# Three graph layers on one core: the subset counts of a table lookup move behind the lookups, on half of the array's rows, with their bias as a row of ones

## The chip, the cores and the metric

The kernel runs on one core of a Trainium2 chip. The metric is the device time of one execution in microseconds (us); lower is better. A core has five engines with a queue of instructions each: TensorE (PE in the profile; its weight loads are PEld), VectorE (DVE), ScalarE (ACT), GpSimd (POOL) and SyncE (SP). An engine takes its own instructions in order and waits on semaphores for the others.

## The reference

A batch of 16 graphs with 1024 nodes and 128 features goes through four layers, each followed by a residual sum and a layer norm.

```python
x = _layernorm(x + _L0_gnn_ref(x, adj, ...))   # masked attention
x = _layernorm(x + _L1_gnn_ref(x, adj, W, b))  # largest edge message
x = _layernorm(x + _L2_gnn_ref(x, adj, ...))   # sum over neighbours, two-layer network
x = _layernorm(x + _L3_gnn_ref(x, adj, ...))   # edges thinned row by row, three convolutions
```

The change lies in layer 1. There every node i wants, for each of 128 features, the largest q over its neighbours j:

```python
p = jnp.einsum('bnd,do->bno', x, W1 - W2)
q = jnp.einsum('bnd,do->bno', x, W2)
pre = p[:, :, None, :] + q[:, None, :, :] + b
h = jax.nn.relu(pre) * adj[..., None]
return jnp.max(h, axis=2)
```

## The kernel before

**The lookup.** The 1024 possible neighbours of a graph are cut into groups of six (`GS`). For each group the kernel holds a table with the largest q of each of the 64 subsets of the group. For a node, the subset that its edges pick is found as a one-hot column of 64, and a product of the table with that column looks the value up. Two groups (a pair, `PS` = 12 neighbours) share the 128 rows. A graph has 86 pairs (`NP`). One pair is a *slot*, and a slot has two *half slots*, one for each 512 nodes. 16 graphs make 1376 slots and 2752 half slots; they are the main loop, and everything else of layers 0 to 2, and the thinning of edges for layer 3, is fitted in between as background work.

**One half slot** (`slot`, lines 849 to 892) issues, in this order of the program:

- `look_up` (L830): four products on TensorE for this slot. Each uses 64 of the 128 rows of the array: rows 0 to 63 for one group, 64 to 127 for the other. First both products with the table's `high` part, then both with its `low` part (a value is the sum of two parts). They fill a tile `pg`, of which there are two.
- the background: `dilate_on` and `advance` emit pieces of other streams on TensorE, then on ScalarE, VectorE and GpSimd. A planner with costs and due times (`ROOM`, `ask`) chooses them.
- `low_part` (L819), in the first half of odd slots only: a product that subtracts `high` from the exact table in the tile `pt`; ScalarE then copies `low` out (L821).
- `count` for two slots ahead (L799, L800): a product of the pattern `lit` (+1 and -1) with the 120 rows of adjacency columns `AT` counts, for each of 64 subsets, how well a node's edges fit it; ScalarE makes the one-hot `hot` of it with a Relu whose bias is `one_less` (L800).
- `table` (L811, L814), in the second half of even slots only: two transposes put the next two tables into `pt`, and ScalarE copies `high` out.
- VectorE's `tensor_max` (L890): the running largest value, over the 1024 looked-up elements of each partition.

The order is written out by hand for TensorE, ScalarE, VectorE and GpSimd (`manual_schedule`), so each engine executes what is named above in the order in which the program names it.

**Tiles that matter.** `pm` (a count) and `pt` (a table) share one tag of PSUM with two buffers, `subset`: every new `pm` or `pt` waits until the last but one has been read. From an even slot on the sequence is pm, pm, pt, pm, pm, so the second count of an odd slot takes the buffer that `pt` leaves, and `pt` is left when ScalarE has copied `low`. `AT` has four buffers of 120 rows in fp8; GpSimd issues the load of a chunk (120 columns of adjacency, ten slots' worth) two chunks ahead.

Of the kernel before, what the change touches and what calls it, by code (L numbers as in the profile page):

```python
# [29 lines left out]
F32 = mybir.dt.float32  # L30
F32R = mybir.dt.float32r
BF = mybir.dt.bfloat16
F8 = mybir.dt.float8e4
F16 = mybir.dt.float16
AF = mybir.ActivationFunctionType
# [4 lines left out]
B, N, D, H2 = 16, 1024, 128, 256  # L40
P = 128
T = N // P
GS = 6
PS = 2 * GS
PC = 10
CH = PC * PS
NP = -(-N // PS)
TG = 12
R, G = 32, 4
# [11 lines left out]
def subset_tables():  # L61

    half = P // 2
    s = np.arange(half)
    lit = np.zeros((CH, PC, P), np.float32)
    for j in range(CH):
        a, k = divmod(j % PS, GS)
        lit[j, j // PS, a * half:(a + 1) * half] = np.where((s >> k) & 1, 1.0, -1.0)
    size = sum((s >> k) & 1 for k in range(GS))
    return lit, np.tile(1.0 - size, 2).astype(np.float32).reshape(P, 1)  # L70


@with_exitstack
def tile_graph_layers(ctx: ExitStack, tc, a, out):
    nc = tc.nc
    x, adj, adjT = a["x"], a["adj"], a["adjT"]
    halves = (slice(0, 512), slice(512, 1024))

    consts = ctx.enter_context(tc.tile_pool(name="consts", bufs=1))
# [7 lines left out]
    def bank(name, dtype=F32):  # L87
        return psum.tile([P, 2048 // (2 if dtype == BF else 4)], dtype, tag="bank", name=name, bufs=2)
# [13 lines left out]
    nc.vector.memset(ones_b, 1.0)  # L102
    mhalf = consts.tile([P, T], F32, name="mhalf")
    nc.vector.memset(mhalf, -0.5)
    lit = consts.tile([CH, PC, P], F8, name="lit")
    nc.gpsimd.dma_start(out=lit, in_=a["lit"])
    less = consts.tile([P, P], F32R, name="less")
    nc.vector.tensor_scalar_mul(less, ident, -1.0)
    one_less = consts.tile([P, 1], F32, name="one_less")
    nc.sync.dma_start(out=one_less, in_=a["one_less"])  # L110

    def weight(name, shape=(P, P), how=None, pool=consts):
        t = pool.tile(list(shape), F32, name="w_" + name)
# [49 lines left out]
    pm = bank("pm")  # L163
# [5 lines left out]
    for b in range(B):  # L169
        q, g = divmod(b, G)  # L170
        nc.gpsimd.dma_start(out=half_rows[g * R:(g + 1) * R, :, q],
                            in_=a["nodemask"][b].rearrange("(k r) -> r k", r=R))
# [65 lines left out]
    def layers_012():  # L238
# [4 lines left out]
        apool = es.enter_context(tc.tile_pool(name="apool", bufs=1))  # L243
# [18 lines left out]
        def ask(engine, cost, take=False, give=False, same=False, delay=0.5, after=None, third=False, urgent=False):  # L262
            return engine, cost, take, give or urgent and None, 0 if same else delay, after, third
# [17 lines left out]
        def columns_of(dst, src, first=0.5):  # L281
            for h in range(2):
                yield ask("PE", 0.44, take=True, delay=0.5 if h else first)
                p = shared("ptr")
                for t in range(4):
                    nc.tensor.transpose(p[:, t * P:(t + 1) * P], src[:, 4 * h + t, :], ident)
                yield ask("A", 0.59, give=True, same=True)
                nc.scalar.copy(dst[:, halves[h]], p)
# [12 lines left out]
        def scores(b):  # L301
# [50 lines left out]
            yield from columns_of(xT, X[b])  # L352
            q = w4.tile([P, NP * PS], F32, name="q", bufs=2)
            nc.gpsimd.memset(q[:, N:], LOWEST)
# [104 lines left out]
        def tables_of(b):  # L459

            if b:
                yield ask("V", 0, urgent=True, after=("tables", b - 1))
            for g0 in range(0, NP, TG):
                n_g = 2 * min(TG, NP - g0)
                yield ask("V", 0.01, same=True, urgent=True, after=("q", b))
# [23 lines left out]
        def dilation():  # L489
# [134 lines left out]
            for k in range(K):  # L624
# [52 lines left out]
                for g in range(G):  # L677
                    nc.sync.dma_start(out=hit_p[g * R:(g + 1) * R],
                                      in_=hit_d.rearrange("(q g) n m -> g n q m", g=G)[g])
                yield (B * NP - 10) / K - 34.43, 0, False  # L680
                hit_T = dil.tile([P, Q, R], BF, name="hit_T")
# [62 lines left out]
        def load_columns(at):  # L744
            b, c = divmod(at, T + 1)
            if b < B:
                rows = min(CH, N - c * CH)
                t = AT[at] = apool.tile([CH, N], F8, name="AT", bufs=4)
                if rows < CH:
                    nc.gpsimd.memset(t, 0.0)  # L750
                nc.gpsimd.dma_start(out=t[:rows], in_=adjT[b, c * CH:c * CH + rows])

        An, AT, subs, qs, ps, values, exps, bests, hots, tables = ({} for _ in range(10))
        now, taken, given, held = 0, 0, {}, {}
        pending = {}
# [6 lines left out]
        def start(stream, first=False):  # L762
            pending[stream] = [next(stream, None), -9]
            streams.insert(0 if first else len(streams), stream)
# [27 lines left out]
        def count(s, h):  # L792

            b, g = divmod(s, NP)
            c, r = divmod(g, PC)
            if h == 0:
                hots[s] = w2.tile([P, N], F32R, name="hot", bufs=3)
            pm = psum.tile([P, 512], F32, tag="subset", name="pm", bufs=2)
            nc.tensor.matmul(pm, lit[:, r, :], AT[b * (T + 1) + c][:, halves[h]], start=True, stop=True)  # L799
            nc.scalar.activation(hots[s][:, halves[h]], pm, AF.Relu, bias=one_less)  # L800

        def table(s):

            b, g = divmod(s, NP)
            g0 = g - g % TG
            assert ("sub", b, g0) in happened, (s, [(x.__name__, pending[x]) for x in streams], room)
            pt = psum.tile([P, 512], F32, tag="subset", name="pt", bufs=2)[:, :2 * P]
            if g + 2 - g0 == min(TG, NP - g0):
                happened["used", b, g0] = now
            for k in range(2):  # L810
                nc.tensor.matmul(pt[:, k * P:(k + 1) * P], subs[b, g0][:, g - g0 + k, :], ident, is_transpose=True,  # L811
                                 start=(k == 0), stop=(k == 1))
            high = w2.tile([P, 2 * P], F32R, name="high", bufs=2)
            nc.scalar.copy(high, pt)  # L814
            tables[s] = pt, high
# [8 lines left out]
        def look_up(s, h, pg):  # L824

            at = s % 2
            for k, part in enumerate(tables[s - at]):
                for a in range(2):
                    rows = slice(64 * a, 64 * a + 64)
                    nc.tensor.matmul(pg[:, a], part[rows, at * P:(at + 1) * P], hots[s][rows, halves[h]],  # L830
                                     start=(k == 0), stop=(k == 1))
# [17 lines left out]
        def slot(s, last):  # L849

            nonlocal now
            now = s
            b, g = divmod(s, NP)
            if s >= 0 and g == 0:
                finish(b)
                if b + 1 < B:
                    start(tables_of(b + 1), True)
                    load_x(b + 1)
                    start(attend(b + 1))
                    start(scores(b + 1))  # L860
                if b:
                    start(rest(b - 1))
            if s >= 0 and g % PC == 0:
                load_columns(b * (T + 1) + g // PC + 2)
            for h in range(2):
                now = s + 0.5 * h
                for e in ROOM:
                    room[e] = min(room[e] + ROOM[e] / 2, ROOM[e])
                if s >= 0:
                    pg = psum.tile([P, 2, 512], F32, tag="wide", name="pg", bufs=2)  # L870
                    look_up(s, h, pg)
                early = s >= 0 and due < now
                if early:
                    dilate_on()
                advance(("PE",))
                advance(("A", "V", "Pool"))
                if s >= 0 and not early:
                    dilate_on()
                if h == 0 and s % 2 and s + 1 < last:
                    low_part(s + 1)  # L880
                if s + 2 < last:
                    count(s + 2, h)
                    if h and s % 2 == 0:
                        table(s + 2)
                if s >= 0:
                    own = bests[b][:, :, halves[h]]
                    if g == 0:
                        nc.vector.tensor_copy(own, pg)
                    else:
                        nc.vector.tensor_max(own, own, pg)  # L890
            if s >= 0:
                hots.pop(s)
# [1 line left out]
        dilate = dilation()  # L894
        due, wants_bank = 0.0, False
        load_x(0)
        for at in range(2):
            load_columns(at)
        front, back = scores(0), attend(0)
        for t in range(T):  # L900
            while ("e", 0, t) not in happened:
# [6 lines left out]
        first = tables_of(0)  # L908
# [9 lines left out]
        last = rest(B - 1)  # L918
# [214 lines left out]
    for b in range(B):  # L1133
        x0 = sb.tile([P, T, D], F32, name="h", bufs=2)
        nc.sync.dma_start(out=x0, in_=x3[b])
        part = load_share(b)
        m = expanded(ahead[b][0])
        transposed(R3[b], x0)
        r = sage(b, convolve(x0, m, part), R3[b], None, weights)
        if b + 1 < B:  # L1140
            start = len(nc.cur_bb.bb.instructions)
# [15 lines left out]
    r = second(0)  # L1157
    for b in range(B):
        near = ep.tile([P, T, N], F8, name="near", bufs=2)
        nc.sync.dma_start(out=near, in_=kept[b])  # L1160
        part = load_share(b)
        following = second(b + 1) if b + 1 < B else None
        pass_on(b, 1, r, expanded(near), part, stats)
        r = following
# [3 lines left out]
    r = second(0)  # L1168
    for b in range(B):
        following = second(b + 1) if b + 1 < B else None  # L1170
        columns(b, r, stats)
        r = following
# [16 lines left out]
    o = summed(0)  # L1189
    for b in range(B):  # L1190
# [17 lines left out]
        o = following  # L1208
# [25 lines left out]
```

## Time and profile before

| | |
|---|---|
| time, median of 3 runs | 6459.39 us (6446.67 to 6460.74) |
| the profiled execution's own time | 6458.95 us |
| its span, and around it | 6457.2 us; 1.75 us |
| main loop, first lookup to last comparison | 132 to 5169 us of the span |
| granted TensorE clock, mean of the span | 0.934 |
| L890 `best<-best,pg` on DVE | 2720 times, mean 1215 ns |
| L800 `hot<-pm,one_less` on ACT | 2752 times, mean 689 ns |
| L799 `pm<-AT,lit` on PE | 2752 times, mean 404 ns |
| L830 `pg<-hot,high` and `pg<-hot,low` on PE | 5504 times each, mean 519 and 411 ns |

The profile comes from one execution. A TensorE row's duration runs from its start to the end of its results; the next product begins before that, so what a product costs in a row of products is the distance from its start to the next start.

### The profile page before, as it was taken

To read this page: it belongs to the slowest core of one execution; us is meant where nothing else is said; L and a number is where in the kernel's file an instruction comes from. 1 tells how busy PE (TensorE), PEld (TensorE's weight loads), DVE (VectorE), ACT (ScalarE), POOL (GpSimd) and SP (SyncE) were. 2 spreads that over 40 slices of the span, in tenths; PEclk is the share of its full clock that TensorE was granted. 3 is DMA by queue.
4 is the path that set the end of the run, shared out by engine and by line. 5 is a ranking of instruction groups with operands and counts; after the bars stand their busy time and mean duration, and the time that the engine had idled before them with its cause. 6 is when DMAs were issued, how large, how long until landed. Compare 5 with 4: busy or idle time off the path is not lost. (4 is left out here: it accounts for less than half of the span.)

```text
span 6457.2 us, 90620 instructions
## 1 busy us (share of the span) xinstructions
PE 5729.3 (89%) x29184; PEld 2962.2 (46%) x29354; DVE 4978.8 (77%) x7877; ACT 3946.3 (61%) x7142; POOL 3502.1 (54%) x11319
## 2 busy tenths in 40 slices
PE   6989999989899999999989998989998867877998
PEld 3444444444444444444444444444443335555654
DVE  3888888888888888888888888888888834444445
ACT  4667666666667666766666666666665623333755
POOL 2665766666666666766666666666666511110113
PEclk8989899999899999999999999998998988888999
DMA  5121212121212121212121212121211065654545
GB/s 38 13 30 21 35 21 36 21 34 21 34 21 37 20 35 20 34 20 32 24 34 20 34 20 34 20 35 20 35 21 18 20 101 106 126 103 111 206 167 186
DMA packets 478402, 317.32 MB, mean 49 GB/s; under 512 B 301162, under 2 KB 429668, under 8 KB 473828
## 3 DMA queue, kind: packets, MB, share of 16 engines
q0 software_dynamic: 105648, 84.20, 15.0%
q1 hardware_dynamic: 367600, 226.13, 11.9%
q8 instruction: 230, 3.77, 0.2%
q10 hardware_dynamic: 4676, 1.19, 0.1%
q14 instruction: 248, 2.03, 0.1%
HBM read 412.71 MB, written 117.18 MB: 82 GB/s over the span
## 5 line engine op out<-in xcount | busy, mean ns | idle before, releaser
L890 DVE TENSOR_TENSOR best<-best,pg 128x1024 f32<-128x1024 f32 x2720 | 3258.7, 1215 | 556.8 <-PE pg L830 546.8
L800 ACT ACTIVATE hot<-pm,one_less 128x512 fp32r<-128x512 f32 x2752 | 1882.7, 689 | 736.9 <-PE pm L799 727.5
L830 PE MATMUL pg<-hot,high 64*128 64x512 f32 x5504 | 1436.1, 519 | 239.2 <-DVE best L890 231.4
L830 PE MATMUL pg<-hot,low 64*128 64x512 f32 x5504 | 1139.8, 411 | 0.0
L799 PE MATMUL pm<-AT,lit 120*128 120x512 fp8e4 x2752 | 1110.3, 404 | 20.9 <-ACT hot L800 8.5
L830 PEld LDWEIGHTS pg<-hot,high 64*128 64x128 f32 x5504 | 533.6, 191 | 1018.9 <-DVE best L890 510.5
L830 PEld LDWEIGHTS pg<-hot,low 64*128 64x128 f32 x5504 | 553.0, 198 | 0.0
L658 POOL TENSOR_SCALAR sc<-low_counts,half_mask,rest 16x1 f32<-16x1 f32 x992 | 351.8, 355 | 323.7 <-DVE rest L644 218.8
L799 PEld LDWEIGHTS <-lit 120*128 120x128 fp8e4 x2752 | 272.6, 99 | 520.5 <-issue 460.2
L663 POOL TENSOR_SCALAR sc<-sc 16x1 f32<-16x1 f32 x992 | 397.3, 401 | 105.1
L821 ACT CAST low<-pt 128x256 fp32r<-128x256 f32 x688 | 256.1, 372 | 258.2 <-PE pt L819 255.0
L1039 POOL TENSOR_TENSOR length<-length,mhalf 128x8 f32<-128x8 f32 x48 | 78.9, 1644 | 570.8 <-DVE length L1038 570.8
L660 POOL TENSOR_SCALAR sc<-sc 16x1 f32<-16x1 f32 x992 | 315.0, 318 | 107.7
L819 PE MATMUL pt<-high,less 128*128 128x256 f32 x688 | 294.1, 427 | 85.0 <-ACT high L814 78.2
L703 POOL TENSOR_SCALAR shifts<-centre 128x4 f32<-128x4 f32 x32 | 10.5, 327 | 656.9 <-DVE width L699 633.6
L665 POOL TENSOR_SCALAR hit<-V,sc 16x31 bf16<-16x31 bf16 (+30 forms) x992 | 361.1, 364 | 0.0
L666 POOL TENSOR_SCALAR last_rank<-V,sc 16x31 f32<-16x31 bf16 (+30 forms) x992 | 344.5, 347 | 0.0
L996 ACT CAST m<-near 128x1024 fp32r<-128x1024 fp8e4 x256 | 253.4, 1044 | 112.6 <-DVE near L965 59.6
L475 DVE TENSOR_TENSOR sub<-sub,q 128x24 f32<-128x24 f32 (+11 forms) x768 | 303.3, 396 | 24.0 <-ACT q L297 10.4
L811 PE MATMUL pt<-ident,sub 128*128 128x128 f32 x1376 | 286.1, 291 | 26.7 <-ACT hot L800 22.3
L385 PE MATMUL pav<-v,eT 128*128 128x128 f32 x2048 | 301.7, 293 | 2.1 <-ACT eT L378 2.1
L1009 PE MATMUL pagg<-m,high 128*128 128x512 f32 x768 | 277.3, 432 | 13.2 <-ACT high L1002 13.2
(268 smaller groups left out, 9754.6 us busy)
## 6 DMA issues: line engine op xcount, KB each, us to landing
removed<-gone SPq DMA_DIRECT2D x128, 256.0 KB
An<-in_adj_dram POOLq DMA_DIRECT2D x16, 1024.0 KB, 14.8
E<-in_adj_dram POOLq DMA_DIRECT2D x128, 128.0 KB, 5.8
gone_all<-removed POOLq DMA_DIRECT2D x64, 256.0 KB, 12.3
near<-in_adjT_dram POOLq DMA_DIRECT2D x16, 1024.0 KB, 17.9
kept<-near SPq DMA_DIRECT2D x16, 1024.0 KB
share<-share SPq DMA_DIRECT2D x32, 512.0 KB
hidden<-r SPq DMA_DIRECT2D x32, 512.0 KB
```

The costliest lines, as they stand in the source:

```text
L385: nc.tensor.matmul(pav, eT[:, c, :], values[b][:, c, :], start=(c == 0), stop=(c == T - 1))
L475: nc.vector.tensor_max(sub[:, :n_g, n:2 * n], sub[:, :n_g, 0:n], qg[:, 2 * g0:2 * g0 + n_g, k:k + 1].to_broadcast([P, n_g, n]))
L658: gp.tensor_scalar(half, mine, half_mask[:, m], rest[:, n:n + 1], op0=ALU.mult, op1=ALU.add)
L660: gp.tensor_scalar(sf, half, 5.5, sf, op0=ALU.is_gt, op1=ALU.mult)
L663: gp.tensor_scalar(to, at, sf, none, op0=ALU.subtract, op1=ALU.subtract)
L665: gp.tensor_scalar(hit[:, n, n + 1:], V[:, n, n + 1:], at, None, op0=ALU.is_equal)
L666: gp.tensor_scalar(last[:, n + 1:], V[:, n, n + 1:], to, None, op0=ALU.is_le)
L799: nc.tensor.matmul(pm, lit[:, r, :], AT[b * (T + 1) + c][:, halves[h]], start=True, stop=True)
L800: nc.scalar.activation(hots[s][:, halves[h]], pm, AF.Relu, bias=one_less)
L819: nc.tensor.matmul(pt, less, high, start=False, stop=True, skip_group_check=True)
L830: nc.tensor.matmul(pg[:, a], part[rows, at * P:(at + 1) * P], hots[s][rows, halves[h]], start=(k == 0), stop=(k == 1))
L890: nc.vector.tensor_max(own, own, pg)
```

## The change

The count moves from behind the background to directly behind the lookups of the same half slot, on TensorE and on ScalarE. The 120 rows of a chunk are laid out as two parts, in rows 0 to 59 and 64 to 123, in bf16; rows 60 and 124 hold ones, and the matching rows of `lit` hold what the bias was. So a count is a product over 61 rows, rows 0 to 60 or 64 to 124, and the Relu has no bias. `AT` becomes two fixed tiles (`columns_in`), loaded one chunk ahead instead of two, by two DMAs a chunk instead of one. `low_part` and `table` stay where they were.

```diff
-    lit = consts.tile([CH, PC, P], F8, name="lit")
+    lit = consts.tile([P, PC // 2, P], BF, name="lit")
     nc.gpsimd.dma_start(out=lit, in_=a["lit"])
+    for part in range(2):
+        nc.gpsimd.dma_start(out=lit[64 * part + SUB:64 * part + SUB + 1],
+                            in_=a["one_less"].rearrange("(o r) m -> o r m", o=1))
...
-                t = AT[at] = apool.tile([CH, N], F8, name="AT", bufs=4)
-                if rows < CH:
-                    nc.gpsimd.memset(t, 0.0)
-                nc.gpsimd.dma_start(out=t[:rows], in_=adjT[b, c * CH:c * CH + rows])
+                t = AT[at] = columns_in[at % len(columns_in)]
+                for part in range(-(-rows // SUB)):
+                    first = c * CH + part * SUB
+                    n = min(SUB, N - first)
+                    nc.gpsimd.dma_start(out=t[64 * part:64 * part + n], in_=adjT[b, first:first + n])
+        columns_in = [apool.tile([P, N], BF, name=f"AT{i}") for i in range(2)]
+        for t in columns_in:
+            nc.vector.memset(t, 1.0)
...
-            nc.tensor.matmul(pm, lit[:, r, :], AT[b * (T + 1) + c][:, halves[h]], start=True, stop=True)
-            nc.scalar.activation(hots[s][:, halves[h]], pm, AF.Relu, bias=one_less)
+            part, r = divmod(r, PC // 2)
+            rows = slice(64 * part, 64 * part + SUB + 1)
+            nc.tensor.matmul(pm, lit[rows, r, :], AT[b * (T + 1) + c][rows, halves[h]], start=True, stop=True)
+            nc.scalar.activation(hots[s][:, halves[h]], pm, AF.Relu)
...
-                load_columns(b * (T + 1) + g // PC + 2)
+                load_columns(b * (T + 1) + g // PC + 1)
...
                     look_up(s, h, pg)
+                if s + 2 < last:
+                    count(s + 2, h)
...
                 if h == 0 and s % 2 and s + 1 < last:
                     low_part(s + 1)
-                if s + 2 < last:
-                    count(s + 2, h)
-                    if h and s % 2 == 0:
-                        table(s + 2)
+                if h and s % 2 == 0 and s + 2 < last:
+                    table(s + 2)
```

## The prediction

> **What bounds the kernel now.** The summary gives each engine's share of the span; TensorE leads. In the listing by stretches I took the main loop alone, 132 to 5169 us: 5037 us for 2752 half slots, 1.83 us each.
>
> ```profile
> PE 5729.3 (89%) x29184; PEld 2962.2 (46%) x29354; DVE 4978.8 (77%) x7877; ACT 3946.3 (61%) x7142; POOL 3502.1 (54%) x11319
> ```
>
> ```profile
> core 0: us, PE busy (x) PEld busy (x) DVE busy (x) ACT busy (x) POOL busy (x), PEclk, DMA share, GB/s
> 132.00:5169.00 5037.00, 4599.45 (x24024) 2258.00 (x24189) 4366.51 (x6692) 3333.31 (x6297) 3268.80 (x10900) 0.94 0.19 26
> ```
>
> PE is busy 91% of the loop, DVE 87%, ACT 66%, POOL 65%. PE and DVE are coupled by the two `pg` tiles, so either can hold the other. The list of waits over the loop says how often (waiter, releaser, us in total, times, longest):
>
> ```profile
> PE pg L830 <- DVE best L890: 231.4, 238, 5.5
> PE pt L819 <- ACT high L814: 77.7, 231, 11.9
> ...
> PE pt L811 <- ACT hot L800: 22.3, 51, 1.6
> ...
> PE pm L799 <- ACT low L821: 6.7, 12, 1.4
> ...
> DVE best L890 <- PE pg L830: 546.8, 951, 7.7
> ```
>
> DVE waits for PE 547 us, PE for DVE 231 us: PE is the bound most of the time, DVE now and then, and ACT in a small way through the table copies. The timeline of PE prices the steps (start, duration):
>
> ```profile
> 2505.80 0.50 PE L830 MATMUL pg<-hot,high 64*128 64x512 f32 x2
> 2506.14 0.40 PE L830 MATMUL pg<-hot,low 64*128 64x512 f32 x2
> 2506.47 0.39 PE L799 MATMUL pm<-AT,lit 120*128 120x512 fp8e4 x1
> 2506.79 0.50 PE L830 MATMUL pg<-hot,high 64*128 64x512 f32 x2
> 2507.12 0.40 PE L830 MATMUL pg<-hot,low 64*128 64x512 f32 x2
> 2507.45 0.82 PE L427 MATMUL pa<-An,parts 128*128 128x512 fp8e4 x3
> 2508.11 0.38 PE L799 MATMUL pm<-AT,lit 120*128 120x512 fp8e4 x1
> 2508.33 0.38 PE L811 MATMUL pt<-ident,sub 128*128 128x128 f32 x2
> 2508.64 0.50 PE L830 MATMUL pg<-hot,high 64*128 64x512 f32 x2
> ```
>
> Start to start, as medians over the loop: `high` to `low` 0.333 us, `low` to whatever follows 0.326, count to lookup 0.320, but count to transposes 0.22 and the three L427 products 0.216 each. So 512 columns cost 0.216, and each change between 64-row and 128-row products costs 0.10 to 0.11 more. The two products of a pair start 3 ns apart. `high` takes 0.50 where `low` takes 0.40: after a change its weights aren't loaded ahead, another 0.1.
>
> **The count on PE.** In the changed program's order the same pieces stand between two lookups as before, only the count is first. I counted the 2752 gaps: 603 hold nothing but the count, 2146 also background, `low_part` or table transposes, 3 no count.
>
> In the 2146, before: `low` (0.326, with the change) - others - count (0.320, with the change). After: `low` to count 0.216, count to others 0.326, and the last of the others pays 0.1 towards the lookups (two transposes to a lookup: 0.20 for the last, where one is 0.113). Sum of the fixed part: 0.646 before, 0.64 after. Nothing gained. Moving and narrowing the count doesn't make it cheaper.
>
> In the 603, `low` to count falls from 0.326 to 0.216, count to lookup from 0.320 to 0.216, and the next `high` has its weights ahead (0.333 to about 0.22): 0.33 us. It counts only where PE isn't ahead already. By the distance from the release of the `pg` tile to the lookup's start, 253 of them wait for DVE now (0), 281 have over 0.33 us (full), 68 lie between (half): 281 x 0.33 + 68 x 0.165 = 104 us.
>
> No row shows a 61-row product behind a 64-row pair. From below, a product of the same pair starts after 0.003 us; but a pair fills both halves of the rows, so the count has no free half. From above, `high` to `low` 0.333. I take 0.216, the step of equal products, since the 0.333 holds the late weights. At 0.333: 2752 x 0.117 = +322 us; at 0.003: 2752 x 0.213 = -586 us.
>
> The Trainium skill, TensorEngine Tiling (Array Packing), section Overview, promises up to a factor 2 for a contraction of 64 rows or fewer. By it the counts would take half of 0.216, 297 us less; the row with pairs 3 ns apart speaks against it, both halves being taken. The same page, Tiling Modes (Key Properties), says that a change of mode drains the engine. The 0.10 us rows agree; read as one drain saved per half slot it would give 2752 x 0.11 = 303 us, but the order keeps two changes in 2146 of the gaps.
>
> **What ACT no longer holds up.** Before, the Relu (L800) stands on ACT between the background and the table copy `high` (L814), so `low_part` waits. In the 308 gaps where `low_part` directly follows the lookups, lookup to count takes 0.902 on average and 0.556 without a wait (0.326 + 0.230 from the rows): 308 x 0.346 = 107 us. The transposes wait for the Relu of the other `subset` buffer: count to transpose averages 0.301 against 0.221, 662 x 0.08 = 53 us. After, Relus are early; both waits go, apart from halves in which ACT's background is longer than PE's, which I put at 35 us. Gain 125 us.
>
> **The wait that comes instead.** The second count of an odd slot takes the `subset` buffer that `pt` leaves, free when ACT has copied `low` (L821). Before, that count stood at the end of its half slot, and the wait was 6.7 us in all. Now only two pairs of lookups lie between `low_part` and that count, and on ACT the Relu and the background of the first half stand ahead of `low`:
>
> ```profile
> 2508.53 0.69 ACT L800 ACTIVATE hot<-pm,one_less 128x512 fp32r<-128x512 f32 x1
> 2509.11 0.36 ACT L814 CAST high<-pt 128x256 fp32r<-128x256 f32 x1
> 2510.28 0.37 ACT L821 CAST low<-pt 128x256 fp32r<-128x256 f32 x1 [0.80 <-PE pt L819]
> 2510.57 0.69 ACT L800 ACTIVATE hot<-pm,one_less 128x512 fp32r<-128x512 f32 x1
> ```
>
> Here `low` still runs ahead of the Relu. From the first half's lookups, after the change: count at 0.333 + 0.216 = 0.55, its result 0.39 + 0.04 later, Relu step 0.49 (L323, a Relu with no bias; 0.58 with), so ACT's background starts at 1.47. With none, `low` ends at 1.47 + 0.37 + 0.04 = 1.88. PE without background: count to `low_part` 0.326, that 0.23, change 0.1, then lookups 0.55: the second count is due at 1.75. Background on ACT adds its length B, background on PE its length. Of 684 odd slots, by the rows of before:
> - 287 have none on ACT, 189 of them none on PE: 189 x 0.13 = 25 us.
> - 235 copy out what PE made in this half: from PE's end 0.27 + 0.5 + 0.12 (part of a second piece) + 0.41 on ACT against 0.80 on PE: 235 x 0.5 = 118 us.
> - 162 run something else, B 0.74 against 0.25 on PE: about 0.2 + 0.74 - 0.25 = 0.68, 110 us.
>
> Sum 253 us. Queued behind that count on PE are its half's background and the next lookups, for which DVE waits. Where those wait for DVE anyway (some 15%) it costs nothing: 215 us. Ends: 100 us if ACT runs ahead, 290 if nothing is absorbed.
>
> **ACT's background later.** It now starts behind the Relu: exp (L347, 128 times) ends about 0.14 us after PE wants to transpose it, 18 us; with the first count of an odd slot behind a late Relu, and table copies and `rank`, I take 40 us, ends 0 and 100.
>
> **Loads.** GpSimd issues 288 loads instead of 144 and no memset: at 0.55 to 0.66 us about +50 us, beside PE, as POOL is at 65%. A chunk lands in 3.8 us:
>
> ```profile
> AT<-in_adjT_dram POOLq DMA_DIRECT2D x128, 120.0 KB, 3.8
> ```
>
> The lead shrinks to 8 slots, at a graph's end 4 (15 us); cost 0, and without that cover a few us per graph. At the start the row of ones waits for `lit` to land (5.6 us) ahead of the first row load on POOL's queue, whose landing ACT waits for: +4 us, ends 0 and 6.
>
> **Sum.** -104 - 125 + 215 + 40 + 4 = +30 us on the profiled 6458.95 (span 6457.2 and 1.75 around it; the median of the runs, 6459.39, is the same to 0.01%): 6489, say **6490 us**. What a measurement of this kernel can tell from no change is about 0.2%, 13 us.
>
> **Rivals.**
> 1. *Faster: the new wait is mostly covered.* The same 215 us term decides. If ACT's pieces come when PE has as much in the same half, it is 100 us; with the gains whole (104 + 160) and 20 for later background: -140, 6320. For it: ACT idles 727 us waiting for counts, time it gets back, and its Relu is 0.09 us shorter. Against it: in 397 of 684 odd slots a piece on ACT stands ahead of `low`. It decides below about 185 us of stall.
> 2. *Slower still.* 290 us of wait, 100 for late background, and half of the gains: +275, 6735. For it: waits of this kind spread, since a late `low` makes a late count, Relu and background. Against it: ACT is at 66%.
> 3. *The count doesn't join the 64-row mode* (0.333): +322 x 0.85 = +270 and no gain in the 603: 6830.
> 4. *Gain and loss cancel* within 13 us.
>
> **Chances.** Forecast (6473 to 6580) 0.38; slower still, rivals 2 and 3, 0.16; rival 1 0.36, anywhere from 6300 to 6446; rival 4 0.10. So faster 0.36, same 0.10, slower 0.54. The range, 6335 to 6650, leaves out a tenth at each end; the forecast's own is 6473 to 6580.
>
> **What would show it.** Right: PE waiting for ACT's `low` at the count, 150 to 300 us in the list of waits; the waits of `low_part` on `high` and of the transposes on the Relu nearly gone; `low` to count 0.216; count to lookup 0.22 in the 603. Wrong: that wait under 100 us (rival 1), or `low` to count at 0.33 (rival 3).

## The result, and the profile after

The changed kernel takes 6500.68 us (median of 4 runs, 6493.1 to 6513.04), the kernel before 6460.07 us: ratio 1.0067, 95% interval 1.0051 to 1.0084. Slower by 41 us, as forecast (+30, 6490 us). The forecast number came out right; the step that made it did not happen. The rest of this document is about that.

The profiled execution took 6493.1 us, with a span of 6491.1. Its main loop runs from 128.0 to 5200.8 us: 5073 us, 36 more than before (5037). What lies ahead of the loop is 4 us shorter, what lies behind it 2 us longer (1288 before, 1290 after). So the loss is in the loop. First the list of waits of TensorE (PE) there (waiter, releaser, us in total, times, longest):

```profile
PE pg L838 <- DVE best L898: 278.3, 335, 5.1
PE pe L377 <- ACT e L349: 39.1, 66, 1.3
...
PE pt L827 <- ACT high L822: 18.0, 37, 1.2
...
PE pg L838 <- ACT low L829: 5.0, 11, 0.9
```

What was forecast of the other waits is there. `low_part`'s wait for `high` fell from 77.7 to 18 us, the wait of the transposes for the Relu from 22.3 to 1 us; and the wait for exp (`pe <- e`) rose, from 18.6 to 39 us. One thing is not there: no line has the count `pm` waiting for `low`. That wait was to cost 215 us.

So TensorE waits hardly longer than before (without work for 407 us of the loop, before for 438), and yet the loop is longer. The row of the granted TensorE clock in 40 slices, before:

```profile
PEclk8989899999899999999999999998998988888999
```

and after:

```profile
PEclk8989897989899999989889989989887788888999
```

In the 32 slices of the loop, twelve eights instead of six, and three sevens, two of them near its end. The listing by stretches puts it in one number for the loop: 0.94 before, 0.90 now (the column before DMA share):

```profile
core 0: us, PE busy (x) PEld busy (x) DVE busy (x) ACT busy (x) POOL busy (x), PEclk, DMA share, GB/s
132.00:5200.00 5068.00, 4661.32 (x24009) 2403.88 (x24175) 4362.20 (x6686) 3170.59 (x6291) 3335.80 (x11026) 0.90 0.19 30
```

The clock's record knows two values, full and half. Adding up its half-clock spells within the loop gives 563 us in 66 spells before, 1006 us in 81 after. PE has more busy time (4661 us against 4599) for the same products: they are slower, and not more of them.

That this is enough shows when the half slots are parted by the clock under which they begin. Before: 2537 at full clock, 1793 ns each, and 214 at half clock, 2274 ns. After: 2326 of 1771 ns and 425 of 2240 ns. At full clock the change is a gain, 22 ns per half slot; but 211 more half slots, each some 480 ns longer, are 101 us. The gain, 22 ns x 2537, is 56 us. 101 - 56 = 45, against the loop's measured 36.

The timeline of PE after shows the new order, with both kinds of gap (start, duration):

```profile
2505.34 0.40 PE L838 MATMUL pg<-hot,low 64*128 64x512 f32 x2
2505.58 0.39 PE L807 MATMUL pm<-AT,lit 61*128 61x512 bf16 x1
2505.90 0.66 PE L377 MATMUL pe<-ident,e 128*128 128x128 f32 x4
...
2507.47 0.40 PE L838 MATMUL pg<-hot,low 64*128 64x512 f32 x2
2507.71 0.39 PE L807 MATMUL pm<-AT,lit 61*128 61x512 bf16 x1
2507.71 0.62 PE L838 MATMUL pg<-hot,high 64*128 64x512 f32 x2
2507.94 0.62 PE L838 MATMUL pg<-hot,low 64*128 64x512 f32 x2
2508.41 0.39 PE L807 MATMUL pm<-AT,lit 61*128 61x512 bf16 x1
```

`low` to count is 0.24 us, count to background 0.32. In a gap with nothing but a count the next `high` can begin with the count (2507.71 twice), and two lookups' `low` rows are 0.47 us apart; before it was 0.98.

### The profile page after: what moved, and what is told of

The parts are those of the page before. It is cut to its first block, busy times and chain, and to the rows that moved or that the text cites. A ratio compares the mean times of both kernels' runs of the same rounds, so it can differ in the third digit from the quotient of the medians.

```text
span 6491.1 us, 90730 instructions
## 1 busy us (share of the span) xinstructions
PE 5797.8 (89%) x29184; PEld 3111.3 (48%) x29354; DVE 4978.0 (77%) x7879; ACT 3787.2 (58%) x7142; POOL 3572.0 (55%) x11449
## 5 line engine op out<-in xcount | busy, mean ns | idle before, releaser
L808 ACT ACTIVATE hot<-pm 128x512 fp32r<-128x512 f32 x2752 | 1642.5, 597 | 1448.4 <-PE pm L807 1425.8
L838 PE MATMUL pg<-hot,high 64*128 64x512 f32 x5504 | 1542.7, 542 | 298.1 <-DVE best L898 280.2
L838 PE MATMUL pg<-hot,low 64*128 64x512 f32 x5504 | 1258.0, 430 | 5.4 <-ACT low L829 5.0
L807 PE MATMUL pm<-AT,lit 61*128 61x512 bf16 x2752 | 1173.9, 427 | 4.5 <-ACT hot L808 3.5
L838 PEld LDWEIGHTS pg<-hot,high 64*128 64x128 f32 x5504 | 612.3, 200 | 928.6 <-DVE best L898 550.9
L807 PEld LDWEIGHTS <-lit 61*128 61x128 bf16 x2752 | 278.7, 101 | 774.4 <-issue 761.1
L838 PEld LDWEIGHTS pg<-hot,low 64*128 64x128 f32 x5504 | 631.2, 208 | 31.8 <-ACT low L829 18.5
L822 ACT CAST high<-pt 128x256 fp32r<-128x256 f32 x688 | 254.8, 370 | 116.5 <-PE pt L819 115.1
L819 PE MATMUL pt<-ident,sub 128*128 128x128 f32 x1376 | 304.3, 306 | 4.5 <-DVE sub L477 1.2
## 6 DMA issues: line engine op xcount, KB each, us to landing
E<-in_adj_dram POOLq DMA_DIRECT2D x128, 128.0 KB, 5.9
```

Of the source, the lines that this page charges most:

```text
L807: nc.tensor.matmul(pm, lit[rows, r, :], AT[b * (T + 1) + c][rows, halves[h]], start=True, stop=True)
L808: nc.scalar.activation(hots[s][:, halves[h]], pm, AF.Relu)
```

## The experiments

What lowers the clock? Call the gate whatever sets the granted clock to full or half. A product in the *64-row mode* uses rows of one half of the array alone (0 to 63 or 64 to 127), as the lookups do; in the *128-row mode* it isn't confined to a half. Four theories: **A**, the gate answers to how many rows the products use; 61 rows instead of 120 look like less work. **B**, the new order makes it. **C**, products of zeros do not count as work. **D**, the 64-row mode makes it. No kernel leaves work out; E6 and E8 add products of zeros. "Half clock" is the sum of half-clock spells in the main loop of the profiled execution, cut at the loop's ends. It comes from one execution; the mean granted clock of all runs of a kernel agrees within 0.007 (the change 0.894 to 0.899, before 0.931 to 0.937). (The expectations of E6, E7 and E8 name 1041 and 857 us for the change and E3: there a spell is counted whole that begins 3 us before the loop's end.)

| kernel | rows, mode, place of the count | half clock, us | half slot at full clock, ns | median, us | ratio to before (95%) |
|---|---|---|---|---|---|
| before | 120, 128-row, end | 563 | 1793 | 6456 to 6464 | 1 |
| the change | 61, 64-row, behind lookups | 1006 | 1771 | 6501 | 1.0067 (1.0051 to 1.0084) |
| E1 | 125, 128-row, behind lookups | 465 | 1757 | 6354 | 0.9841 (0.982 to 0.9863) |
| E2 | 120, 128-row, behind lookups | 530 | 1763 | 6388 | 0.9894 (0.9876 to 0.9912) |
| E3 | 61, 64-row, end | 822 | 1761 | 6397 | 0.9908 (0.9885 to 0.9931) |
| E4 | the change, buffers in strict turn | 1024 | 1829 | 6628 | 1.0265 (1.0247 to 1.0282) |
| E5 | 65, 128-row, behind lookups | 1172 | 1779 | 6541 | 1.0119 (1.0103 to 1.0136) |
| E5 | 97, 128-row, behind lookups | 690 | 1761 | 6410 | 0.9918 (0.9898 to 0.9939) |
| E5 | 125, 128-row, behind lookups | 462 | 1754 | 6345 | 0.9821 (0.9799 to 0.9842) |
| E6 | the change, zeros on the other rows | 499 | 1785 | 6426 | 0.994 (0.9924 to 0.9957) |
| E7 | E3, Relu first | 802 | 1754 | 6399 | 0.991 (0.9892 to 0.9928) |
| E8 | E7, zeros on the other rows | 509 | 1778 | 6392 | 0.9904 (0.9886 to 0.9922) |
| E9 | 125, 128-row, end, Relu first | 506 | 1769 | 6389 | 0.9899 (0.9878 to 0.9921) |

**E1: all rows.** Everything as in the change, but each count uses 125 rows; the pattern, now in fp8, is zero for the other part.

```diff
-    lit = consts.tile([P, PC // 2, P], BF, name="lit")
+    lit = consts.tile([P, PC, P], F8, name="lit")
...
-            part, r = divmod(r, PC // 2)
-            rows = slice(64 * part, 64 * part + SUB + 1)
+            rows = slice(0, 64 + SUB + 1)
```

> The changed kernel, but each count is a product over 125 rows in the 128-row mode instead of 61 rows (the pattern of the other part is zero). Order, Relu and loads as in the changed kernel. Theory A, the clock gate answers to the rows that products use: TensorE's time at half clock in the main loop goes from 1004 us back to about 563 us, as before the change, and the time to 6330 to 6420 us, below the kernel before. Theory B, the clock falls because of the new order: half-clock time stays near 1000 us, and the time rises to 6500 to 6600 us, since the saving in the gaps with nothing but a count goes. Theory C, zero weights do not count as activity: as B.

6354 us, and half clock 465, which is below what it was before: theory A. B and C fall: same order, and the added patterns are zeros. The kernel beats both the change and the one before.

**E2: the order alone.** The kernel before, with its 120 rows, bias and loads; only the place of the count is new.

```diff
                     look_up(s, h, pg)
+                if s + 2 < last:
+                    count(s + 2, h)
...
-                if s + 2 < last:
-                    count(s + 2, h)
-                    if h and s % 2 == 0:
-                        table(s + 2)
+                if h and s % 2 == 0 and s + 2 < last:
+                    table(s + 2)
```

> The kernel before, with only the count moved directly behind the lookups, and the Relu with it: 120 rows in fp8, bias tile, four column buffers as before. Theory A (rows): half-clock time about 563 us, 6350 to 6430 us, faster than before by the table copies that ACT no longer holds up. Theory B (order): half-clock time about 1000 us, 6520 to 6620 us.

6388 us, half clock 530, 33 us less than before. At 120 rows the order doesn't lower the clock, and it is a gain of 1.1%.

**E3: the rows alone.** The change, with the count back at the end of the half slot (the diff of E2 in reverse).

> The changed kernel with the count at its old place, at the end of the half slot; 61 rows, row of ones and loads as in the change. Theory A (rows): half-clock time about 1000 us, and slower than the changed kernel or equal to it, 6520 to 6650 us. Theory B (order): half-clock time about 563 us, 6380 to 6470 us.

Neither: half clock 822, nearer to A, but 6397 us, as B had it, and faster than before. So each half of the change by itself is a gain, and both together a loss. The clock has a part in that: 563, 530, 822, 1006 us for before, E2, E3 and the change. What A had not seen is that 61 rows at the end of the half slot stand directly ahead of the lookups, in the same mode, so that count and `high` begin together in about half of the half slots, and not only in the gaps that hold nothing else:

```profile
2504.51 0.39 PE L807 MATMUL pm<-AT,lit 61*128 61x512 bf16 x1
2504.55 0.58 PE L838 MATMUL pg<-hot,high 64*128 64x512 f32 x2
2504.86 0.50 PE L838 MATMUL pg<-hot,low 64*128 64x512 f32 x2
```

In 1450 of the 2752 half slots of E3 `low` starts under 0.5 us after the count; in the change in 243, before in none.

**E4: the buffer of the missing wait.** The change, with the two `subset` buffers taken in strict turn.

```diff
+        ring, turns = [psum.tile([P, 512], F32, name=f"ring{i}", tag=f"ring{i}") for i in range(2)], [0]
...
-            pm = psum.tile([P, 512], F32, tag="subset", name="pm", bufs=2)
+            pm = next_ring()
...
-            pt = psum.tile([P, 512], F32, tag="subset", name="pt", bufs=2)[:, :2 * P]
+            pt = next_ring()[:, :2 * P]
```

> The changed kernel with the two subset buffers taken in strict turn, as the prediction had it, so that the second count of an odd slot takes the buffer that the table leaves. If the prediction's step was right in its price and wrong only in which buffer is taken: TensorE waits for the copy of low at the count, 150 to 300 us in the list of waits, and the time is 6650 to 6780 us. If the price was wrong too: under 100 us of waits, and within 40 us of the changed kernel.

The list of waits of PE in its loop:

```profile
PE ring L813 <- ACT low L835: 128.4, 256, 1.8
```

6628 us, 127 more than the change. The wait exists when the buffers are forced, at 128 us where 253, or 215 after what is absorbed, had been worked out; it fell between the two expectations.

That the changed program takes another buffer can be read from its own trace. In 389 of 687 odd slots the second count starts before the copy of `low` has ended; in E4 and in the kernel before, it does so in none. Beside the count at 2505.58, shown above, ScalarE still copies `low`:

```profile
2505.42 0.36 ACT L829 CAST low<-pt 128x256 fp32r<-128x256 f32 x1
```

Nor does that count ever start before the Relu of the first count has ended; in the kernel before, it does so 323 times. So it takes the Relu's buffer now, and took the one that `pt` leaves before.

**E5: only the number of rows.** All counts start at row 0 and run in the 128-row mode; 65, 97 or 125 rows, the added ones with zero patterns against ones. The three kernels differ in one number, 65 in the lines here; their columns lie in four tiles, one for each part.

```diff
...
-            rows = slice(64 * part, 64 * part + SUB + 1)
-            nc.tensor.matmul(pm, lit[rows, r, :], AT[b * (T + 1) + c][rows, halves[h]], start=True, stop=True)
+            rows = slice(0, 65)
+            nc.tensor.matmul(pm, lit[rows, r, :], AT[b * (T + 1) + c][part][rows, halves[h]], start=True, stop=True)
```

> The changed kernel's order, loads and Relu, with the counts always from row 0 and over 65 rows, so that they run in the 128-row mode (65 rows do not fit in 64); four column tiles in fp8. Its pair, the next kernels, differ only in that number: 97 and 125 rows, with zeros as patterns. Theory A (the clock gate answers to rows in use): half-clock time in the main loop near 1000 us, 6480 to 6580 us. Theory D (the 64-row mode, or its mixing with 128-row products, lowers the clock): near 500 us and the same time as with 125 rows, about 6355 us.

> As the one before, with 97 rows. Theory A: half-clock time between the two others, 650 to 850 us, and 6400 to 6480 us. Theory D: as with 125 rows.

> As the one before, with 125 rows. Both theories: half-clock time near 500 us and 6340 to 6380 us, like the kernel with 125 rows and the two parts side by side (6354 us).

The listing by stretches, 65, 97 and 125 rows in turn; read PE's busy time (first after the comma) and the clock (third from the right):

```profile
132.00:5050.00 4918.00, 4577.33 (x23316) 2278.72 (x23316) 4200.94 (x6479) 3038.78 (x6071) 3235.93 (x10684) 0.89 0.19 26
```

```profile
132.00:5050.00 4918.00, 4514.29 (x23915) 2257.34 (x23916) 4303.79 (x6628) 3109.76 (x6228) 3309.78 (x10940) 0.93 0.19 27
```

```profile
132.00:5050.00 4918.00, 4468.93 (x24159) 2240.94 (x24159) 4336.87 (x6680) 3141.23 (x6292) 3338.14 (x11023) 0.95 0.19 27
```

The same instructions but for that number, 0.89, 0.93, 0.95. In the same stretch the kernel with the slowest clock gets through the fewest products (23316 against 24159) and is the busier for it. Half clock is 1172, 690 and 462 us, the time 6541, 6410 and 6345 us: A. D falls, since no count of these three runs in the 64-row mode (`low` to count is 0.326 us in all of them, the step with a change, against 0.24 in the change). The price of the clock: the loops of 65 and 125 rows are 5118 and 4927 us, 191 us for 711 us more at half clock, 0.27 us for each.

**E6: full rows in the 64-row mode.** Beside each count a product of zero weights on the other 61 rows, added to the lookup that uses those rows.

```diff
+        def beside(s, h, pg):
...
+            a = 1 - r // (PC // 2)
+            rows = slice(64 * a, 64 * a + SUB + 1)
+            nc.tensor.matmul(pg[:, a], nothing[rows], AT[b * (T + 1) + c][rows, halves[h]], start=False, stop=True)
...
                     count(s + 2, h)
+                    if s >= 0:
+                        beside(s + 2, h, pg)
```

> The changed kernel, 61 rows in the 64-row mode, with a product of zero weights over the other 61 rows directly behind each count, added to the lookup that uses those rows (it adds zero). Theory A: the two start within some ns of each other and cost the time of one; rows in use double, half-clock time goes from 1041 to about 500 us, and the time to 6280 to 6400 us. It costs VectorE up to 0.22 us later lookups. Theory D: half-clock time stays near 1000 us and the time at 6500 us or above.

```profile
2504.06 0.40 PE L840 MATMUL pg<-hot,low 64*128 64x512 f32 x2
2504.30 0.39 PE L849 MATMUL pg<-AT,nothing 61*128 61x512 bf16 x1
2504.30 0.39 PE L809 MATMUL pm<-AT,lit 61*128 61x512 bf16 x1
2504.62 0.39 PE L829 MATMUL pt<-high,less 128*128 128x256 f32 x1
```

The added product costs PE no time (`low` to count 0.24, count to the next 0.32, as without it), and the clock is back, half clock 499 us, as A had it and D not. The stretch that read 0.89 to 0.95 in E5 has 0.95 here:

```profile
132.00:5050.00 4918.00, 4434.38 (x26517) 2233.50 (x26517) 4304.18 (x6610) 3124.47 (x6199) 3293.30 (x10880) 0.95 0.19 30
```

The time, 6426, is 26 over the expectation: every lookup is ready later, and PE waits 348 us for VectorE's comparison instead of 278:

```profile
PE pg L840 <- DVE best L910: 348.2, 457, 5.0
```

**E7, E8, E9: the old place, looked at more closely.** E7 is E3 with the Relu of the last count emitted first in the next half slot (`one_hot`, the lines here); E8 is E7 with the zero product, which here opens the next lookup's sum; E9 is E7 with E1's rows.

```diff
                     look_up(s, h, pg)
+                one_hot()
                 early = s >= 0 and due < now
```

> The kernel with 61-row counts at the old place (6397 us, half-clock time 857 us), with the Relu of each count emitted first in the next half slot on ScalarE. If ScalarE's order is what the change gained: the waits of the transposes and of low_part go and the time falls by 30 to 90 us, to 6310 to 6365 us. If the gain of moving the count came from TensorE's order: 6380 to 6400 us. Half-clock time near 860 us in both.

> The one before, with a product of zero weights over the other 61 rows beside each count; it opens the next lookup's sum with zeros, so VectorE does not wait for it. Theory A (the clock gate answers to rows in use): half-clock time falls from about 860 to about 520 us, and the time by 50 to 100 us, to 6240 to 6320 us. If the other half of the rows was of use to the high products that start beside a count: the fall is eaten up, 6320 to 6400 us at the lower half-clock time.

> Counts over 125 rows in the 128-row mode at the old place, the Relu first in the next half slot. Against the 61-row kernel with the same order it tells what the 64-row mode is worth just ahead of the lookups: half-clock time about 520 us; if the mode is worth nothing there, 6320 to 6370 us, like 125 rows behind the lookups (6345 to 6354 us); if a count and the high products really overlap in the 64-row mode, 6380 to 6430 us.

E7: 6399 against 6397, no difference, so the Relu's place on ScalarE alone gains nothing there. E8: half clock falls from 802 to 509, the time by nothing that counts (6392); at full clock its half slot is 24 ns longer (1778 against 1754). Its lookups beside a count look like this:

```profile
2506.76 0.39 PE L809 MATMUL pm<-AT,lit 61*128 61x512 bf16 x1
2506.76 0.39 PE L815 MATMUL pg<-AT,nothing 61*128 61x512 bf16 x1
2506.80 0.59 PE L852 MATMUL pg<-hot,high 64*128 64x512 f32 x2
2507.22 0.39 PE L852 MATMUL pg<-hot,low 64*128 64x512 f32 x2
```

There `low` starts 0.46 us behind the count, in E7 0.34 (medians at full clock), as the expectation had it if the zeros take rows that `high` can use. PE's longer wait for VectorE (289 against 263 us) has a part too. E9: 6389, ten less than E7 with 296 us less at half clock, which at 0.27 us each are 80 us; so ahead of the lookups the 64-row mode saves about 70 us, an estimate, and loses them by the clock. With full rows the place behind the lookups is the better one (6345 to 6354).

## Why the prediction was right, and where it was not

- **What bounds the kernel:** right. PE carries the loop; what slows PE slows the kernel.
- **The count on PE in the 2146 gaps with other work:** right in the sum. `low` to count 0.238 (0.216 taken), count to others 0.32 (0.326). No gain there: these gaps' mean, `low` to `low`, went from 1976 to 2028 ns, which is the clock: those that begin at full clock have 1941 and 1938. E2, with the order alone, has 1934 over all.
- **The 603 gaps with only a count:** the term was 104 us. Their mean fell from 1313 to 1184 ns, 129 ns x 602 = 78 us. Where PE doesn't wait, the saving was larger than thought (985 to 475 ns, not 0.33 us), and more of them ended in a wait for VectorE (359 instead of 253).
- **What ACT no longer holds up:** 125 us. The two waits went, but in the lists they are 81 us, 100 before and 19 after. E2, which has this and none of the narrower rows, shortens the loop by 70 us, some 9 of them by the clock; with the 40 us taken for later background the prediction had 85. E7 says that it isn't the Relu's early place alone.
- **The wait that comes instead: 215 us, and measured nothing.** This is the step that failed, "the second count of an odd slot takes the `subset` buffer that `pt` leaves". In the changed program it takes the other one, as the 389 counts that start ahead of the end of `low`'s copy show. Turns were counted, which is right for the kernel before. A rule that fits both kernels is that the pool hands out the buffer that is released first in the program's order: with the Relu ahead of the copy of `low` on ScalarE, that is the Relu's. No run tests this rule by itself. E4 forces the predicted buffer and finds 128 us of wait and 127 us of time, so the price of 215 us was also 1.7 times what it is.
- **Its place was taken by the clock**, which no step and no rival had. 443 us more at half clock, at E5's 0.27 us, are 119 us. Without them the change would stand 83 us below the loop before, an estimate.
- **Loads and start:** no cost in the loop was found in the change (E1 waits 13.9 us for a load, E6 7.4); the start was 4 us shorter, not longer.
- **The rivals:** none of the four described what happened. The time that rival 3 states, 6830, doesn't follow from its terms: 270 more without the 104 us of gain is 6863. That the forecast's number, sign and range hold is luck: an imagined loss of 215 us stood where 119 us of another kind came, and the gains, 189 us net of the late background, were about 105 too high.

**Open:** why at 61 rows the place of the count changes the clock (822 and 802 us at the end, 1006 behind the lookups), when at 120 and 125 rows it moves it by 33 and 44 us (563 and 530; 506 and 462). And why, at full clock, the half slots of the change (1771 ns) are no shorter than E1's (1757) in spite of the 64-row mode's saving.

## What to carry to other kernels

In this kernel a product over fewer rows took the same time and still cost: where TensorE is the bound, read the granted clock before and after, and compare half slots at equal clock, before any story of waits is believed. What narrowing an operand costs in clock can be won back by filling the idle rows with zeros, as in E1, E5 and E6; whether it pays depends on who else could use those rows (E8). And where a pool chooses buffers, look up which buffer an instruction gets; a count of turns by hand is a guess.

## What the runs showed of the hardware that was not expected

The gate follows the rows in use. E5 shows it with nothing else changed, and rows of zero weights against constant ones count too. A tally from the traces says how: for each 3.41 us of the loop, columns streamed times the share of the 128 rows, over what steps of 0.216 us for 512 columns would bring (fp32 products counted twice, as their steps are twice as long, but the lookups once). The stretches at full clock after which the gate closed have a median of 0.31 in the kernel before and 0.31 in the changed one; those after which it stayed open 0.72 and 0.69. Over all 13 kernels the two medians are 0.28 to 0.32 and 0.66 to 0.76. The level at which the gate closes hasn't moved; the work of the whole loop has, from 0.64 to 0.58.

The Trainium skill, TensorE: Matmul & The Clock Gate, Part 1, says that the gate knows half and full clock and looks at windows of 3.4 us; the records agree (0.5 and 1.0 only, spells of whole multiples of 3.41 us). It speaks of idle gaps as the cause. Here PE was idle for less of the loop after the change than before (407 us in 5068, 438 in 5037), and the clock fell. The same page, Why this matters for your kernels, says that a product over 32 rows takes the time of one over 128; E5 agrees (0.23 us from the count to the next product at 65, 97 and 125 rows alike) and adds the price in clock.

Two 61-row products on different halves of the rows start in the same hundredth of a microsecond (E6), and a count and the `high` products behind it nearly so (E3), when they share the 64-row mode.
